# A two-layer Flamingo block on one core: the transfers that turn x, in rows of 2048 bytes and from GpSimd's queue

## The chip, the cores and the metric

The kernel runs on one core of a Trainium2 chip. The core has engines that work side by side: TensorE (PE) multiplies matrices, VectorE (DVE) and ScalarE (ACT) work elementwise, GpSimd (POOL) takes small rest work, and SyncE (SP) mostly asks for transfers. A transfer is asked for in the instruction stream of some engine and then carried out by 16 DMA engines that the core has. Each engine works through its own instructions in order, so an instruction that waits holds up all that are behind it.

The metric is the device time of one execution in microseconds (us), here the median of three runs. The profile is of one further execution, whose own time is given beside its span.

## The reference

Eight batches of 512 tokens, 512 features each, in float32 throughout. Two layers, each a gated cross-attention and a gated feed-forward part, all four with a layer norm in front and a residual around:

```python
x = x + tanh(g_xattn[0]) * L0_xattn(layernorm(x), ctx, Wq, Wg, bg, Wkv, Wo)      # "xa0"
x = x + tanh(g_ffn[0])   * L0_ffn(layernorm(x), proj1, b1, proj2, b2, gate_w)    # "ff0"
x = x + tanh(g_xattn[1]) * L1_xattn(layernorm(x), ctx, mask)                     # "xa1"
x = x + tanh(g_ffn[1])   * L1_ffn(layernorm(x), gate, gate_up, down, ...)        # "ff1"
```

- L0_xattn is linear attention with 16 heads over 64 context tokens, gated by a sigmoid: projections of 512 x 512.
- L0_ffn is a GELU network 512 to 2048 to 512 (its argmax over gate_w is thrown away).
- L1_xattn has no projections: softmax(x ctx^T / sqrt(512)) ctx, with a mask over the 64 context tokens.
- L1_ffn is a mixture of experts: a router of 32 logits a token, top 8, renormalised; the experts are merged into 8 groups of width 192, all of which are computed for each token and summed with the token's group weights.

## The kernel before

**Products.** Every large product is done by a scheme of seven block products in place of eight (Winograd's form of Strassen's), on blocks of half the rows and half the columns. The weights' block combinations are made once and kept in DRAM; those of x, called S, are made by four DVE sums per block (`token_combinations`, L686 to L689). `Up` (matmuls at L910) multiplies a layer's input by the first weights, with quarters of the turned x (`xnT`) or of S as the moving operand, 256 columns at a time. `SplitDown` (matmuls at L1105) does the second product of both feed-forward parts, with the scheme applied twice, and leaves its sums in PSUM; ACT copies them out (`part_ff_down`, L1132 and L1133) and DVE adds them up and on to x.

**Stages.** The stages run one after the other, each over the eight batches: xa0 (to about 377 us), ff0 (377 to 1085 us), and one stage for the second layer, in which each batch goes through xa1 and then ff1 (1085 us to the end, with a period of some 112 us). While PE works on one block, the next block is prepared, in steps of a generator that the main loop calls: `prep_ff0(b)`, or `prep_ff1(b)`, which is `cross_attention(b)` and then the norm, the router and its weights.

**The part that is changed.** A feed-forward product needs x normalised and turned, features on the partitions. `normed` (from L476) makes it:

1. DVE takes mean and variance of each quarter of the tokens (`bn_stats`, `st`, L487; `bn_aggr`, L488) and two small values from them (L490, L494).
2. POOL makes `rstd` (L495) and `nshift` (L497), 128x4 each.
3. ACT writes `xn` = x * rstd + nshift, a quarter of the tokens at a time (L507), with the columns regrouped.
4. DVE turns squares of 32 x 32 within each quarter of `xn`, in place (L562).
5. Sixteen transfers from SBUF to SBUF, for each group `q` of 32 partitions and each `l` of four column groups, carry a block of 32 partitions to partitions `32 l` and on of `xnT` (L580). Nothing of this is computed; it is a move across partitions.

The first blocks (xa0 and ff0_0) are turned on PE instead (L524, L528). The others, that is ff0_1 to ff0_7, and xa1 and ff1 of all eight batches, 23 in all, go by the sixteen transfers: 368 transfers of 64 KB. In the profile they are called `xnT_ff` and `xnT_xa` and have line L580, or L60 where a wrapper records the instruction in its written order.

Who uses `xnT`: the S sums (L686 to L689), `Up`'s products (L910), the scores of xa1 (`pst`, L729, 8 matmuls a batch), and the router's logits (`plt`, L789, 32 small matmuls a batch). From `plt` ACT copies the logits (`lT`, L797), PE turns them (`pl`, L800), DVE picks the top 8, and POOL and DVE make the group weights (`wg_e`, L825; `w`, L828; `pw`, L832).

**Order and queues.** The program is handed to a scheduler, which decides each engine's order by its own reckoning of durations, except where an engine is in the set `in_order`: then the instruction keeps its place in the written program. `with here("gpsimd")` puts GpSimd in that set for a statement. In ff0 the set holds SyncE alone; from the first step of the second layer on it is empty, and the scheduler orders SP too. SP asks for these in ff0 and ff1: weights in tiles of 256 KB into a ring of 16 tiles (`w_ff<-ff_up` for `Up`, `w_ff_down<-stream_ff` for `SplitDown`; `load_steps`, L1493 and L1498), x of the block after next (`x_ff<-x_ff`), the shares (group weights spread over rows, L850), the stores of the result, and the sixteen transfers per block:

```python
with here("gpsimd"):
    nc.sync.dma_start(out=xnT[ts(l, HD), :, q, :], in_=xn[ts(q, HD), :, ts(l, P)])
```

POOL asks for three transfers a batch in ff1 (`ctxd` twice, the context's rows, and `ctxdT`), and computes `rstd`, `nshift` and `wg_e`.

Of the kernel before, what the change touches and what calls it, by code (L numbers as in the profile page):

```python
# [30 lines left out]
P = 128  # L31
# [4 lines left out]
HD = 32  # L36
# [32 lines left out]
def flamingo_kernel(  # L69
# [405 lines left out]
    def normed(ph, b, tag, normed_part=lambda t: None):  # L475

        xb = xs[ph, b]
        by_products = ph == "xa0" or tag == "ff0_0"
        xnT = work.tile([P, NC, S] if ph == "xa0" else [P, NT, NC, P], F32, tag="xnT", name=f"xnT_{tag}")
        mv = small.tile([P, NT, 2], F32, tag="mv", name=f"mv_{tag}")  # L480
        held = ph == "ff0" and b > 1
        by_scalar = tag != "xa0_0"
# [32 lines left out]
        if by_products:  # L515

            def normed_tile(t):
                xn[t] = bank["xn"].tile([P, D], F32, tag="xn", name=f"xn_{tag}_{t}", bufs=2)
                norm(t, xn[t])

            def turn(t):
                pt = psum(f"pt_{tag}_{t}").rearrange("p (c q) -> p c q", q=P)
                for c in range(NC):
                    nc.tensor.transpose(pt[:, c, :], xn[t][:, ts(c, P)], ident)  # L524
                if ph == "xa0":
                    nc.scalar.copy(xnT[:, :, ts(t, P)], pt)
                else:
                    nc.scalar.copy(  # L528
                        xnT[:, t].rearrange("p q (c i) -> p c q i", c=NC),
                        pt.rearrange("p c (q i) -> p c q i", q=NC),  # L530
                    )

            if ph == "xa0" and b == 0:
                normed_tile(0)
                normed_tile(1)
                yield
                for t in range(NT):
                    turn(t)
                    if t + 2 < NT:
                        normed_tile(t + 2)  # L540
                    yield
                return xnT
            if ahead:
                normed_tile(0)
                yield
            for t in range(NT):
                if not ahead:
                    normed_tile(t)
                elif t + 1 < NT:
                    normed_tile(t + 1)  # L550
                turn(t)
                normed_part(t)
                yield
            return xnT


        at = (0, 2, 1, 3) if tag.startswith("ff1") else range(NT)
        xn = bank["xn"].tile([P, NT, D], F32, tag="xn", name=f"xn_{tag}")

        def squares(t):  # L560
            with here(*(["vector"] if ahead else [])):
                nc.vector.transpose(xn[:, at[t], :], xn[:, at[t], :])  # L562
            normed_part(t)

        for t in range(NT + 1):
            if t < NT:
                norm(
                    t,
                    xn[:, at[t], :].rearrange("p (l c e) -> p c l e", l=NC, c=NC),
                    lambda of: of.rearrange("p (c l e) -> p c l e", l=NC, c=NC),  # L570
                )
            if t > 0:
                squares(t - 1)
            if t % 2:
                yield
        yield
        for q in range(NC):
            for l in range(NC):
                with here("gpsimd"):
                    nc.sync.dma_start(out=xnT[ts(l, HD), :, q, :], in_=xn[ts(q, HD), :, ts(l, P)])  # L580
        yield
        if ph == "ff1":
            for _ in range(3):
# [3 lines left out]
    def features_of(ph, xnT):  # L587

        if ph == "xa0":
            return xnT.rearrange("p c (g i) -> p c g i", i=HD)  # L590
        return xnT.rearrange("p t q (c i) -> p c (t q) i", c=NC)

    turned = [dram.tile([P, NC, M], F32, tag=f"turned{b}", name=f"turned_{b}") for b in range(B)]

# [84 lines left out]
    def token_combinations(ph, b, xnT):  # L679

        s = work.tile([P, 4, 2, H2], F32, tag="S", name=f"S_{ph}_{b}", bufs=1)
        v = features_of(ph, xnT)
        a11, a12 = v[:, 0:2, 0:8], v[:, 2:4, 0:8]
        a21, a22 = v[:, 0:2, 8:16], v[:, 2:4, 8:16]
        to = s.rearrange("p k c (g i) -> p k c g i", i=HD)
        nc.vector.tensor_tensor(to[:, 0], a21, a22, ALU.add)  # L686
        nc.vector.tensor_tensor(to[:, 1], to[:, 0], a11, ALU.subtract)
        nc.vector.tensor_tensor(to[:, 2], a11, a21, ALU.subtract)
        nc.vector.tensor_tensor(to[:, 3], a12, to[:, 1], ALU.subtract)  # L689
        return s  # L690

    def prep_ff0(b):
        xb = xs["ff0", b]
# [9 lines left out]
    def cross_attention(b):  # L703
# [23 lines left out]
        for c in range(NC):  # L727
            for r in range(2):
                nc.tensor.matmul(  # L729
                    pst[ts(r, M), :],  # L730
                    lhsT=ctxT[:, c, :],
                    rhs=features_of("ff1", xnT)[:, c].rearrange("p (u r q) i -> p r u q i", u=2, r=2)[:, r],
                    start=c == 0,
                    stop=c == NC - 1,
                )
# [46 lines left out]
    def prep_ff1(b):  # L782
# [4 lines left out]
        for c in range(NC):  # L787
            for t in range(NT):
                nc.tensor.matmul(  # L789
                    plt[ts(t, E), :],  # L790
                    lhsT=router_sb[:, c, :],
                    rhs=features_of("ff1", xnT)[:, c, ts(t, NC)],
                    start=c == 0,
                    stop=c == NC - 1,
                )
# [92 lines left out]
    class Up(Unit):  # L888
# [6 lines left out]
        def product(self, m, p):  # L895
# [3 lines left out]
            for n in range(2):  # L899
                for c in range(2):  # L900
                    moving = {
                        1: v[:, c, 0:8],
                        2: v[:, 2 + c, 0:8],
                        4: v[:, 2 + c, 8:16],
                        5: s[:, 0, c, :],
                        6: s[:, 1, c, :],
                        7: s[:, 2, c, :],
                        3: s[:, 3, c, :],
                    }[m]
                    nc.tensor.matmul(  # L910
                        p[:, n, :],
# [742 lines left out]
```

## Time and profile before

| | |
|---|---|
| Time, median of 3 runs | 2036.1 us (2035.9 to 2041.35) |
| The profiled execution's own time | 2034.87 us |
| Its span; mean granted clock | 2033.1 us; 0.999 |
| PE busy | 2003.0 us, 99% |
| DVE busy | 1512.3 us, 74% |
| ACT busy | 646.7 us, 32% |
| POOL busy | 95.9 us, 5% |
| Queue q1 (what SP asks for) | 349616 packets, 479.79 MB, 73.6% |
| Queue q0 (what POOL asks for) | 1584 packets, 3.57 MB, 0.7% |

By stage, PE busy within each stretch (us):

| stretch | length | PE busy | DVE busy | DMA share |
|---|---|---|---|---|
| 60 to 350 (xa0) | 290.0 | 286.98 | 235.55 | 0.58 |
| 350 to 470 (into ff0) | 120.0 | 114.99 | 84.25 | 0.80 |
| 470 to 1085 (ff0) | 615.0 | 610.58 | 438.37 | 0.87 |
| 1085 to 1200 (first batch of layer two) | 115.0 | 108.46 | 89.22 | 0.82 |
| 1200 to 1980 (the other batches) | 780.0 | 778.86 | 595.92 | 0.80 |
| 1980 to 2033 (the end) | 53.0 | 47.09 | 41.98 | 0.55 |

How to read it: the busy time of an engine is the sum of its instructions' spans, with instructions that only ask for a transfer left out, so SP has no busy time at all and POOL's does not include its asking. Weight loads (PEld) lie beside matmuls. The share of a DMA queue is the time that its packets took over that of 16 engines for the whole span. Lines that name a group of instructions give line, engine, operation, and `out<-in` by the program's names; after `x` the number of instructions. A line of waits gives the engine and tile that waited, what ended the wait, and then the total in us, how many times, and the longest.

### The profile page before, as it was taken

The numbers are of one execution on the slowest core, as the hardware profiler recorded it, in microseconds if no ns is written. First come the engines' busy times: TensorE is split into PE (matmuls) and PEld (weight loads), VectorE is DVE, ScalarE is ACT, GpSimd is POOL, SyncE is SP. The second block draws the span as 40 slices with busy tenths as digits, with TensorE's granted clock in tenths as the row PEclk, the third lists the DMA queues.
The fourth block names the chain that finished last, engine by engine and source line by source line (L and its number), as shares of the span: only waits on it lengthen the run. The fifth ranks groups of instructions, "written<-read, shape, count | busy, mean of one in ns | idle before, by whom it ended". The sixth has DMA issues, their size and how long they took to land.

```text
span 2033.1 us, 34969 instructions
## 1 busy us (share of the span) xinstructions
PE 2003.0 (99%) x12428; PEld 1778.0 (87%) x12428; DVE 1512.3 (74%) x3012; ACT 646.7 (32%) x1294; POOL 95.9 (5%) x147
## 2 busy tenths in 40 slices
PE   9999999999999999999999999999999999999998
PEld 5888887889989899999988989898989888898988
DVE  4788888675857677777857787787778686876858
ACT  4533443323242424233233331313222232313122
POOL 3000000000000000000001010000001010100000
PEclk9999999999999999999999999999999999999999
DMA  7376556688979898989877869787878878786865
GB/s 211 127 217 189 178 156 175 231 304 276 341 236 347 264 341 260 314 291 297 305 245 233 294 217 294 230 291 212 294 238 266 262 234 273 215 288 211 277 203 172
DMA packets 357228, 508.79 MB, mean 250 GB/s; under 512 B 42944, under 2 KB 156768, under 8 KB 352960
## 3 DMA queue, kind: packets, MB, share of 16 engines
q1 hardware_dynamic: 349616, 479.79, 73.6%
q10 hardware_dynamic: 5856, 23.20, 3.1%
q0 software_dynamic: 1584, 3.57, 0.7%
q8 instruction: 100, 1.64, 0.3%
q14 instruction: 72, 0.59, 0.1%
HBM read 413.04 MB, written 69.27 MB: 237 GB/s over the span
## 4 chain that ended last, share of the span: by engine, by line
PE 47%; DVE 1%; DMA 1%; SPq 1%; ACT 0%; issue 0%; POOL 0%; DVEq 0%; POOLq 0%
PE x_ff L910 16%; PE w_ff L910 8%; PE x_ff_down L1105 7%; PE w_ff_down L1105 5%; PE z_ff L910 4%; PE z_ff_down L1105 2%; PE v_ff_down L1105 2%; PE pst L729 1%; PE pr L774 1%; SPq L580 0%; PE plt L789 0%; DMA w_ff<-ff_up 0%; DMA x_ff<-x_ff 0%; DVE xn_ff L562 0%; DVE st_xa L487 0%
## 5 line engine op out<-in xcount | busy, mean ns | idle before, releaser
L910 PE MATMUL w_ff<-S_ff,w_ff 128*128 128x256 f32 x1280 | 305.4, 380 | 2.7 <-DVE up_ff L1003 1.2
L910 PE MATMUL x_ff<-S_ff,w_ff 128*128 128x256 f32 x1280 | 304.0, 379 | 0.0
L910 PE MATMUL x_ff<-xnT_ff,w_ff 128*128 128x256 f32 x1280 | 299.1, 381 | 0.4 <-ACT u_ff L922 0.4
L922 ACT COPY u_ff<-x_ff 128x512 f32<-128x512 f32 x240 | 139.9, 583 | 463.4 <-PE x_ff L910 427.1
L910 PEld LDWEIGHTS w_ff<-S_ff,w_ff 128*128 128x128 f32 x1280 | 240.8, 190 | 39.5 <-DVE up_ff L1003 3.0
L910 PEld LDWEIGHTS x_ff<-S_ff,w_ff 128*128 128x128 f32 x1280 | 242.5, 190 | 34.2 <-ACT a_ff L60 0.8
L910 PEld LDWEIGHTS x_ff<-xnT_ff,w_ff 128*128 128x128 f32 x1280 | 240.4, 191 | 34.2 <-issue 1.8
L1105 PE MATMUL x_ff_down<-w_ff_down,split_ff_down 128*128 128x128 f32 x1344 | 161.8, 275 | 0.0
L1105 PEld LDWEIGHTS x_ff_down<-w_ff_down,split_ff_down 128*128 128x128 f32 x1344 | 155.8, 192 | 0.0
L910 PE MATMUL z_ff<-xnT_ff,w_ff 128*128 128x256 f32 x640 | 152.8, 380 | 0.0
L1119 DVE TENSOR_TENSOR part_ff_down<-part_ff_down 128x128 f32<-128x128 f32 x315 | 83.9, 285 | 73.2 <-ACT part_ff_down L1132 64.2
L910 PEld LDWEIGHTS z_ff<-xnT_ff,w_ff 128*128 128x128 f32 x640 | 119.9, 190 | 19.9 <-issue 4.5
L1105 PE MATMUL w_ff_down<-w_ff_down,split_ff_down 128*128 128x128 f32 x896 | 107.9, 275 | 0.0
L1105 PEld LDWEIGHTS w_ff_down<-w_ff_down,split_ff_down 128*128 128x128 f32 x896 | 103.9, 192 | 0.0
L970 ACT ACTIVATE a_ff<-a_ff,b_sb 128x256 f32<-128x256 f32 x128 | 58.1, 501 | 91.9 <-DVE a_ff L965 91.9
L1105 PE MATMUL w_ff_down<-w_ff_down,s_ff 128*128 128x128 f32 x672 | 83.1, 275 | 2.6 <-ACT part_ff_down L1132 2.6
L965 DVE TENSOR_TENSOR a_ff<-w_ff,u_ff 128x512 f32<-128x512 f32 x64 | 43.9, 685 | 53.8 <-ACT u_ff L922 53.2
L1105 PEld LDWEIGHTS w_ff_down<-w_ff_down,s_ff 128*128 128x128 f32 x672 | 80.1, 192 | 3.6 <-ACT part_ff_down L1132 2.8
L1003 DVE TENSOR_TENSOR up_ff<-w_ff,u_ff 128x512 f32<-128x512 f32 x96 | 65.6, 683 | 23.6 <-ACT u_ff L922 23.3
L1105 PE MATMUL x_ff_down<-w_ff_down,a_ff 128*128 128x128 f32 x672 | 82.8, 275 | 0.0
L1105 PEld LDWEIGHTS x_ff_down<-w_ff_down,a_ff 128*128 128x128 f32 x672 | 79.5, 192 | 0.4
L993 DVE SCALAR_TENSOR_TENSOR g_ff<-th_ff,x_ff 128x512 f32<-128x512 f32 x48 | 32.6, 680 | 63.2 <-ACT th_ff L992 63.2
(262 smaller groups left out, 3266.7 us busy)
## 6 DMA issues: line engine op xcount, KB each, us to landing
w_ff_down<-stream_ff SPq DMA_DIRECT2D x680, 256.0 KB
w_ff<-ff_up SPq DMA_DIRECT2D x560, 256.0 KB
stream_ff<-build_ff_down SPq DMA_DIRECT2D x49, 448.0 KB
x_ff<-x_ff SPq DMA_DIRECT2D x16, 1024.0 KB
share<-shares SPq DMA_DIRECT2D x64, 256.0 KB
xnT_ff<-xn_ff SPq DMA_DIRECT2D x240, 64.0 KB
ff_up<-build_ff_up SPq DMA_DIRECT2D x42, 256.0 KB
x_ff<-x_xa ACTq DMA_DIRECT2D x8, 1024.0 KB
```

The lines of the kernel that those rows point to most:

```text
L729: nc.tensor.matmul(pst[ts(r, M), :], lhsT=ctxT[:, c, :], rhs=features_of("ff1", xnT)[:, c].rearrange("p (u r q) i -> p r u q i", u=2, r=2) ...
L774: nc.tensor.matmul(pr[t], lhsT=eT[half, t // 2, :], rhs=c2[half, :], start=True, stop=True)
L910: nc.tensor.matmul(p[:, n, :], lhsT=w[:, c, ts(n, P)], rhs=moving, **self.mark(m, 2 * n + c),)
L922: nc.scalar.copy(self.s[m], p)
L965: nc.vector.tensor_tensor(h, p, s, ALU.add)
L970: nc.scalar.activation(h[:, n, :], p[:, n, :], AF.Gelu, bias=b1_sb[:, f : f + 1])
L993: nc.vector.scalar_tensor_tensor(g, th, 1.0, p, ALU.add, ALU.mult)
L1003: nc.vector.tensor_tensor(u, p, s, ALU.add)
L1105: nc.tensor.matmul(p[bank][:, place, :], lhsT=operand[k][:, c, :], rhs=w[at // 4][:, ts(at % 4, P)], start=bank not in opened, stop=True, ...
L1119: return lambda: nc.vector.tensor_tensor(m(k), m(k), m(by), ALU.add)
```

## The change

`xn` and `xnT` are laid out anew so that what one of the sixteen transfers reads in a partition lies in one row of 2048 bytes, and what it writes too; before, it was four rows of 512 bytes at each end. The token quarter moves from the first to the second place in `xnT` ([column group, token quarter, 128]) and in `xn`. All that reads `xnT` or S is rewritten to find the same elements: the views of `features_of`, the S sums, the moving operands of `Up`, the scores and the logits. S, for blocks outside of xa0, takes the order of `xnT`. The sixteen transfers are asked for with `nc.gpsimd.dma_start` in place of `nc.sync.dma_start`; the `here("gpsimd")` around them now applies to the engine that asks. No product, sum or transfer is added or left out.

```diff
--- before.py
+++ after.py
@@ -476,7 +476,7 @@
 
         xb = xs[ph, b]
         by_products = ph == "xa0" or tag == "ff0_0"
-        xnT = work.tile([P, NC, S] if ph == "xa0" else [P, NT, NC, P], F32, tag="xnT", name=f"xnT_{tag}")
+        xnT = work.tile([P, NC, S] if ph == "xa0" else [P, NC, NT, P], F32, tag="xnT", name=f"xnT_{tag}")
         mv = small.tile([P, NT, 2], F32, tag="mv", name=f"mv_{tag}")
         held = ph == "ff0" and b > 1
         by_scalar = tag != "xa0_0"
@@ -526,7 +526,7 @@
                     nc.scalar.copy(xnT[:, :, ts(t, P)], pt)
                 else:
                     nc.scalar.copy(
-                        xnT[:, t].rearrange("p q (c i) -> p c q i", c=NC),
+                        xnT[:, :, t].rearrange("p q (c i) -> p c q i", c=NC),
                         pt.rearrange("p c (q i) -> p c q i", q=NC),
                     )
 
@@ -555,18 +555,18 @@
 
 
         at = (0, 2, 1, 3) if tag.startswith("ff1") else range(NT)
-        xn = bank["xn"].tile([P, NT, D], F32, tag="xn", name=f"xn_{tag}")
+        xn = bank["xn"].tile([P, NC, NT, P], F32, tag="xn", name=f"xn_{tag}")
 
         def squares(t):
             with here(*(["vector"] if ahead else [])):
-                nc.vector.transpose(xn[:, at[t], :], xn[:, at[t], :])
+                nc.vector.transpose(xn[:, :, at[t], :], xn[:, :, at[t], :])
             normed_part(t)
 
         for t in range(NT + 1):
             if t < NT:
                 norm(
                     t,
-                    xn[:, at[t], :].rearrange("p (l c e) -> p c l e", l=NC, c=NC),
+                    xn[:, :, at[t]].rearrange("p l (c e) -> p c l e", c=NC),
                     lambda of: of.rearrange("p (c l e) -> p c l e", l=NC, c=NC),
                 )
             if t > 0:
@@ -577,7 +577,7 @@
         for q in range(NC):
             for l in range(NC):
                 with here("gpsimd"):
-                    nc.sync.dma_start(out=xnT[ts(l, HD), :, q, :], in_=xn[ts(q, HD), :, ts(l, P)])
+                    nc.gpsimd.dma_start(out=xnT[ts(l, HD), q], in_=xn[ts(q, HD), l])
         yield
         if ph == "ff1":
             for _ in range(3):
@@ -587,8 +587,8 @@
     def features_of(ph, xnT):
 
         if ph == "xa0":
-            return xnT.rearrange("p c (g i) -> p c g i", i=HD)
-        return xnT.rearrange("p t q (c i) -> p c (t q) i", c=NC)
+            return xnT.rearrange("p c (t q i) -> p c t q i", q=NC, i=HD)
+        return xnT.rearrange("p q t (c i) -> p c t q i", c=NC)
 
     turned = [dram.tile([P, NC, M], F32, tag=f"turned{b}", name=f"turned_{b}") for b in range(B)]
 
@@ -679,15 +679,20 @@
     def token_combinations(ph, b, xnT):
 
         s = work.tile([P, 4, 2, H2], F32, tag="S", name=f"S_{ph}_{b}", bufs=1)
-        v = features_of(ph, xnT)
-        a11, a12 = v[:, 0:2, 0:8], v[:, 2:4, 0:8]
-        a21, a22 = v[:, 0:2, 8:16], v[:, 2:4, 8:16]
-        to = s.rearrange("p k c (g i) -> p k c g i", i=HD)
+        if ph == "xa0":
+            v = features_of(ph, xnT).rearrange("p c t q i -> p c t (q i)")
+            a11, a12, a21, a22 = (v[:, ts(h, 2), ts(r, 2)] for r in range(2) for h in range(2))
+            to = s.rearrange("p k c (t i) -> p k c t i", t=2)
+        else:
+            a11, a12, a21, a22 = (xnT[:, :, ts(r, 2), ts(h, 2 * HD)] for r in range(2) for h in range(2))
+            to = s.rearrange("p k c (q t i) -> p k (c q) t i", q=2, t=2)
         nc.vector.tensor_tensor(to[:, 0], a21, a22, ALU.add)
         nc.vector.tensor_tensor(to[:, 1], to[:, 0], a11, ALU.subtract)
         nc.vector.tensor_tensor(to[:, 2], a11, a21, ALU.subtract)
         nc.vector.tensor_tensor(to[:, 3], a12, to[:, 1], ALU.subtract)
-        return s
+        if ph == "xa0":
+            return to.rearrange("p k c t (q i) -> p k c t q i", i=HD)
+        return to.rearrange("p k q t (c i) -> p k c t q i", c=2)
 
     def prep_ff0(b):
         xb = xs["ff0", b]
@@ -729,7 +734,7 @@
                 nc.tensor.matmul(
                     pst[ts(r, M), :],
                     lhsT=ctxT[:, c, :],
-                    rhs=features_of("ff1", xnT)[:, c].rearrange("p (u r q) i -> p r u q i", u=2, r=2)[:, r],
+                    rhs=features_of("ff1", xnT)[:, c].rearrange("p (u r) q i -> p r u q i", r=2)[:, r],
                     start=c == 0,
                     stop=c == NC - 1,
                 )
@@ -789,7 +794,7 @@
                 nc.tensor.matmul(
                     plt[ts(t, E), :],
                     lhsT=router_sb[:, c, :],
-                    rhs=features_of("ff1", xnT)[:, c, ts(t, NC)],
+                    rhs=features_of("ff1", xnT)[:, c, t],
                     start=c == 0,
                     stop=c == NC - 1,
                 )
@@ -899,13 +904,13 @@
             for n in range(2):
                 for c in range(2):
                     moving = {
-                        1: v[:, c, 0:8],
-                        2: v[:, 2 + c, 0:8],
-                        4: v[:, 2 + c, 8:16],
-                        5: s[:, 0, c, :],
-                        6: s[:, 1, c, :],
-                        7: s[:, 2, c, :],
-                        3: s[:, 3, c, :],
+                        1: v[:, c, 0:2],
+                        2: v[:, 2 + c, 0:2],
+                        4: v[:, 2 + c, 2:4],
+                        5: s[:, 0, c],
+                        6: s[:, 1, c],
+                        7: s[:, 2, c],
+                        3: s[:, 3, c],
                     }[m]
                     nc.tensor.matmul(
                         p[:, n, :],
```

## The prediction

> **What bounds the kernel now.** I read the page's engine totals first, then the waits of PE, then the groups of the moved transfers, then the stretches by stage.
>
> ```profile
> span 2033.1 us, 34969 instructions
> PE 2003.0 (99%) x12428; PEld 1778.0 (87%) x12428; DVE 1512.3 (74%) x3012; ACT 646.7 (32%) x1294; POOL 95.9 (5%) x147
> q1 hardware_dynamic: 349616, 479.79, 73.6%
> q0 software_dynamic: 1584, 3.57, 0.7%
> ```
>
> PE is busy for 2003.0 of 2033.1 us, and its instructions number the same after the change. So no DMA saving is worth anything by itself; only a PE gap that closes or opens counts. Queue q1, which holds what SP asks for, is busy 73.6% on average: not the limit, though it can be late in places. The waits of PE from 385 us on (before that no x goes by the changed transfers):
>
> ```profile
> PE v_ff_down L1105 <- DMA w_ff_down<-stream_ff: 6.1, 3, 3.0
> PE w_ff_down L1105 <- ACT part_ff_down L1132: 2.6, 1, 2.6
> PE plt L789 <- issue: 1.4, 3, 0.8
> PE w_ff L910 <- DVE up_ff L1003: 1.2, 1, 1.2
> PE w_ff L910 <- DVE x_ff L776: 1.2, 1, 1.2
> PE plt L789 <- DMA xnT_ff<-xn_ff: 0.6, 1, 0.6
> ```
>
> These and smaller ones sum to 14.6 us. Besides, nine matmuls at 1093.5-1097 took 631 ns in place of 379, in the one stretch with a granted clock of 0.99: 9 x 0.25 = 2.3 us. **The whole possible gain is 14.6 + 2.3 = 17 us.** The 6.1 us are the weight waits at 433 (2.6), 623 (0.5) and 1090 us (3.0). What SP did ahead of the first shows in its timeline:
>
> ```profile
> 403.86 0.32 SPq L60 DMA_DIRECT2D w_ff_down<-stream_ff  x1
> 404.23 4.41 SPq L60 DMA_DIRECT2D ff_up<-build_ff_up  x7
> 408.75 11.89 SPq L60 DMA_DIRECT2D xnT_ff<-xn_ff  x16
> 420.74 1.02 SPq L60 DMA_DIRECT2D w_ff_down<-stream_ff  x2
> ...
> 428.39 5.40 SPq L60 DMA_DIRECT2D w_ff_down<-stream_ff  x7
> ```
>
> SP asks for nothing else during 11.89 us of x; the down weights go out late, and PE waits at 433.42. Likewise 16 x issues at 1074.54-1086.10 stand ahead of the down weights of 1087.32, for which PE waits at 1089.76.
>
> **The change, part by part.** (1) *Issues.* 23 preparations (ff0_1 to 7, and xa and ff of eight batches) x 16 = 368 issues leave SP and join POOL.
>
> ```profile
> L60 SPq DMA_DIRECT2D xnT_ff<-xn_ff x128: 585/599/1986, 408.7 to 1085.5; - x128
> L580 SPq DMA_DIRECT2D xnT_ff<-xn_ff x112: 586/599/1609, 1188.1 to 1870.1; - x112
> ```
>
> On SP, 599 ns each, 0.645 from start to start: 16 take 10.3 us or more, and SP gets back 368 x 0.645 = 237 us. On POOL the nearest row is the context load (64 rows of 2 KB; the moved ones have 32):
>
> ```profile
> L60 POOL DMA_DIRECT2D ctxd<-in_ctx x16: 523/556/603, 947.7 to 1770.3; - x16
> DMA to landing us min/median/max: 2.8/4.2/6.3
> ```
>
> So 16 x 0.56 = 9.0 us of issuing a preparation, 206 us in all on an engine busy for 95.9. What then stands behind it on POOL: in a batch of ff1 the next block's rstd_xa and nshift_xa (1302.14, 1.2 us), which now come after the 16 of xnT_ff, near 1309-1310. ACT uses them at 1313.17 (xn_xa), so some 2 us of slack cover it; without the cover ACT's xn_xa, and behind it the copy of the router's logits, are late by the excess. wg_e (1319.24) follows still later.
>
> (2) *Rows.* In the trace's packet records those of 512 B took 27 ns (median; mean 30.9), of 2048 B 84 (mean 98): 47104 x 30.9 becomes 11776 x 98, 1455 to 1154 us over 16 engines, 91 to 72 each, 0.9% of their share. Hidden; worth nothing but a little earlier landing.
>
> (3) *Layouts.* The moving operand now has 128 B runs with other strides. A matmul from xnT (strided already) takes 381 or 379 ns and one from S (contiguous) 380 or 379; DVE's S sums 681 and transposes 704, ACT's xn 805, with the same element counts after. I cost this at 0. If strides cost 5 ns on each of the 1280 + 640 matmuls from xnT, it would be 10 us; the equal rows exclude that.
>
> (4) *ff0, 377-1085 us.* PE's order stays. POOL can issue when the transposes end (near 390 us for ff0_1) with landing by 399-406; first use is 428.9: hidden, with 20 us of cover. SP's 11.89 us go away before 433. I take both waits as closed: **-2.6 - 0.5 = -3.1 us** (ends 0 and -3.1).
>
> (5) *Turn from ff0 to ff1, 970-1100.* Here SP without its 16 issues asks for weights and x about 10 us sooner. The waits of the cluster at 1087-1097 (0.8 plt, 3.0 w_ff_down, 0.7 small ones, and the 2.3 us of slow matmuls, which follow the gaps) sum to 6.8; 10 us of head start exceed each of them, and I take **-6.0** (ends 0 and -6.8). At 1009.87 PE waits 2.6 us for a copy behind four xn_xa in a row on ACT (1009.06-1011.99); in the built order two of that bank's copies come between them, so that at most two stand together: half, **-1.3** (ends 0 and -2.6). The gaps at 1065.68 and 1190.6 (1.2 each) hang on DVE: 0. Against it: the scheduler, reckoning with the earlier SP, moves DVE's statistics st_xa_0 14 to 25 instructions ahead, before the sum at 974.5. They need x_ff, which SP asked for at 977.67 and which let DVE go at 986.19, 8.5 us after. Without the 10.4 us of issues at 964.65 it goes out at 967-972, so landing is 975.6-980: DVE, in order, blocks for 1 to 5 us, with a_ff and s_ff sums behind it that PE multiplies by. st_xa_1 is moved alike, before 1075.8, with x asked for at about 1071-1075. DVE is busy only 74%, so most is made up: **+1.5 for both** (ends 0 and +8).
>
> (6) *Steady ff1, seven batches.* A period of 112 us has PE busy for 111.43 to 112.00, so almost no gain is left. The new order wants xnT_xa at about 1269, with POOL able to send it from 1212: 40 us of cover. The tight one is plt, which needs all 16 landings:
>
> ```profile
> 1299.32 0.70 DVE L562 STREAM_TRANSPOSE xn_ff<-xn_ff 128x512 f32<-128x512 f32 x1
> 1313.44 1.08 PE L789 MATMUL plt<-xnT_ff,router_sb 128*32 128x128 f32 x32
> ```
>
> The last transpose ends at 1300.0, plt is three matmuls earlier after the change (0.65 us), so landing has 12.75 us. A queue has eight completion lanes in the built order, so the ninth issue waits for the first to land. With landing L from issue, sixteen are down at the greater of 15 x 0.56 + L and, in two rounds, 2L + 7 x 0.56: 11.2 us for L = 2.8, 12.5 for 4.2, 16.5 for 6.3. By the median row plt is just in time. Before, plt waited 1.15 us over three batches; I take the same after: **0** (ends -1.2, and 7 x 3.7 = +26).
>
> *The rule against it.* The Trainium skill ("DMA: Bandwidth & Descriptors", section "SWDGE vs HWDGE vs iDMA") calls descriptors written by software on GpSimd the slower set-up; the page's first table gives about 1 us to the first byte against 0.6. The trace's nearest rows: plt starts 1.8 to 3.1 us after SP's last x issue ends, so 2.4-3.7 from its start, against 4.2 on POOL; yet the issue itself is shorter, 0.556 to 0.599. Before, plt starts 13.4 us after the last transpose, with waits of at most 0.6: so long do SP's sixteen take. With the rule's 0.4 us for each of two rounds of lanes, and no credit for issuing, POOL's take 14.2: 1.5 us late in each of seven batches, **+10 in place of 0**. I take the row, since L = 4.2 already holds that latency and 0.56 the shorter issue; the rule's answer stays in the range. The page "SBUF - State Buffer" ("Who interferes with whom") further says that GpSimd's descriptor writing is shut out while DVE runs in a two-port mode. DVE's 512-element rows take 650 to 704 ns whatever the operation, none near half, and the context loads kept to 523-603 ns beside DVE at 78%: I add nothing for it.
>
> **Sum:** -3.1 - 6.0 - 1.3 + 1.5 + 0 = -8.9 us against a profiled execution of 2034.87 (span 2033.1 and 1.8 around it), so 2026.0. That execution lies 1.2 us under the median of the three runs, 2036.1; on the median's footing, 2027.2, said as 2027.
>
> **The rivals.** *Late landing on POOL* ends on the other side. Place: plt in each ff1 batch; stalls begin at L = 4.4 us (2 x 4.4 + 3.9 = 12.7) and eat the whole gain at 5.0, where 13.9 is 1.2 too late, x 7 = 8. At L = 6.3, the slowest context load, 3.7 x 7 = 26 us: 2053. For it: 64 KB from only 32 partitions into 32 others may be slower than the context's 64, and DMA share is 0.8. Against: SP's x landed in under 3.7 us in that traffic, with four times the packets. *Waits only change places*: SP is ahead, but w_ff_down waits for ring tiles that PE frees, or DVE's early statistics cost +8 where SP gave -9: 2035. For it: the ring holds 16 tiles however early SP is free. Against: at 408-420 SP was plainly late. *All goes well*: every gap named shuts and DVE doesn't block: -13 to -17, 2019-2023. *Nothing of what it says*, that transfers stay with SP, is excluded: the built order has them on POOL.
>
> **How the numbers follow.** My forecast (2023-2031) 0.47; waits change places (2031-2042) 0.20; late landing (above 2042) 0.18; all goes well (below 2023) 0.15. About 6 us (0.3%) is what a measurement of this kernel can tell from no change, so faster means below 2030: all of the best case and 0.42 of my forecast, whose last us lies above, 0.57. Slower means above 2042: 0.18. The same is the rest, 0.25. The range leaves out 0.1 at each side, the lower part of the best case and the upper part of late landing: 2021 to 2046.
>
> **What would show it.** Right: no w_ff_down wait on stream_ff at 433 and 1090; POOL's xnT issues near 0.56 us; plt waits under 0.5 us a batch; a DVE wait of 1-5 us for x_ff near 975; matmuls from xnT at 379-381 ns. Wrong: plt <- DMA xnT_ff of over 1 us in each batch, POOL issues over 0.7 us, ACT's xn_xa waiting for nshift_xa with the logits behind it, or PE waits on DVE that outgrow 2 us at 975-1100.

## The result: slower, and the profile after

The changed kernel takes 2048.35 us (median of 7 runs, 2041.27 to 2058.18) against 2035.9 (7 runs, 2032.2 to 2041.35). The ratio over all runs is 1.0067, with a 95% interval of 1.0045 to 1.0089 (the medians alone give 1.0061). The forecast was 2027.

The head of the page of the changed kernel, to be held against that of the kernel before (busy times, share of the span, number of instructions; then packets, MB and share of two DMA queues):

```profile
span 2044.1 us, 35151 instructions
PE 2006.4 (98%) x12428; PEld 1781.7 (87%) x12428; DVE 1508.6 (74%) x3012; ACT 648.5 (32%) x1294; POOL 281.1 (14%) x515
q1 hardware_dynamic: 296624, 455.65, 71.2%
q0 software_dynamic: 13360, 27.71, 4.9%
```

The transfers moved as the change says: q0 has the 24 MB more that q1 lost. q1's share fell by 2.4 points, but q0's rose by 4.2. The span grew by 11.0 us all the same. PE is busy 3.4 us longer for the same 12428 matmuls, so the other 7.6 us are idle time of PE. What it waited for after 385 us:

```profile
PE plt L794 <- DMA xnT_ff<-xn_ff: 16.7, 8, 3.7
PE x_ff L915 <- ACT u_ff L927: 2.4, 1, 2.4
PE pw L837 <- DVE w L833: 1.2, 1, 1.2
PE v_ff_down L1110 <- ACT a_ff L975: 1.1, 1, 1.1
PE x_ff_down L1110 <- DVE split_ff_down L1095: 0.9, 1, 0.9
```

(Lines from L910 on are five higher than before: L910 is L915, L789 is L794.) The 6.1 us of waits for `w_ff_down<-stream_ff` are gone, as forecast. In their place stands one line that the kernel before had with 2.0 us: the router's logits wait for x, now in every one of the eight batches.

How the two kernels ran against each other is seen best by a landmark that both have: the end of the last DVE transpose (L562) of each batch's ff1 block, read from the timelines of DVE.

| batch | before, us | after, us | after is ahead by | plt then waited, after |
|---|---|---|---|---|
| 1 | 1188.03 | 1182.47 | 5.6 | 2.3 |
| 2 | 1300.02 | 1297.91 | 2.1 | 0.6 |
| 3 | 1411.75 | 1410.08 | 1.7 | 3.4 |
| 4 | 1523.99 | 1526.70 | -2.7 | 0.5 |
| 5 | 1635.57 | 1638.79 | -3.2 | 1.1 |
| 6 | 1747.36 | 1751.47 | -4.1 | 1.9 |
| 7 | 1859.38 | 1864.96 | -5.6 | 3.7 |
| end | 2033.1 | 2044.1 | -11.0 | |

The changed kernel was 5.6 us ahead when the steady part began, with 3.1 us already lost at the plt of batch 0. Then it lost 16.6 us in seven batches.

One of these batches in the timeline of GpSimd's queue (start, length, instruction; in brackets the idle time before it and what ended it), and then of SyncE's in the same time:

```profile
1527.25 3.99 POOL L60 DMA_DIRECT2D xnT_ff<-xn_ff  x8 [8.22 <-PE x_ff L915]
1532.08 3.92 POOL L60 DMA_DIRECT2D xnT_ff<-xn_ff  x8 [0.84 <-DMA xnT_ff<-xn_ff]
1536.02 1.27 POOL L495 TENSOR_TENSOR rstd_xa<-var_xa,neg_half 128x4 f32<-128x4 f32 x1
1537.37 0.46 POOL L497 TENSOR_TENSOR nshift_xa<-nshift_xa,rstd_xa 128x4 f32<-128x4 f32 x1
```

```profile
1525.67 8.84 SPq L1498 DMA_DIRECT2D w_ff_down<-stream_ff  x6
1535.91 2.04 SPq L1503 DMA_DIRECT2D w_ff<-ff_up  x2
```

Eight issues of 0.50 us, a pause until the first of them has landed, eight more. The last issue starts at 1535.5 and plt starts at 1539.42, 12.7 us after the transposes of 1526.70. Of the seven batches this is the one with the shortest wait at plt, 0.5 us. SyncE asks for six weight tiles (1.5 MB) in the midst of it. The landings of the ff1 blocks on GpSimd, batches 1 to 7:

```profile
L60 POOL DMA_DIRECT2D xnT_ff<-xn_ff x112: 498/498/558, 1183.0 to 1875.8; - x112
...
  DMA xnT_ff<-xn_ff: 8.2, 10
...
  ACT xn_xa L507: 21.6, 6
  PE plt L794: 13.6, 7
...
DMA to landing us min/median/max: 3.2/4.3/6.5
```

The second line is GpSimd's idle time until an earlier transfer of its own has landed, before the ninth issue or one close behind it: its queue has eight completion lanes, each free again when its transfer has landed. The two lines after it are who waited for these landings: PE for 13.6 us, and ACT, whose next xn reuses the buffer that the transfers read, for 21.6. ACT is let go by the same landings; no wait of PE hangs on it.

The 3.4 us of longer busy time come after the longest of these waits. The windows around the plt of batch 3 (us, PE busy, then other engines; PEclk is the granted clock):

```profile
1420.00:1426.00 6.00, 2.61 (x24) 2.03 (x26) 1.74 (x3) 0.69 (x2) 3.16 (x6) 1.00 0.72 199
1426.00:1432.00 6.00, 6.00 (x45) 4.80 (x37) 4.76 (x21) 4.67 (x11) 0.00 (x0) 0.72 0.19 48
1432.00:1438.00 6.00, 6.00 (x30) 5.18 (x29) 4.28 (x11) 0.76 (x2) 4.39 (x7) 1.00 0.65 174
```

After 3.4 us of idling the clock is 0.72 over the next 6 us: 0.28 x 6 = 1.7 us on top of the wait. The same happens at batches 1 and 7 (waits of 2.3 and 3.7), three times in all, 5.1 us; the kernel before had it once (10 us at 0.83, behind the wait of 3.0 at 1090 us), 1.7 us. The difference is the 3.4 us. With the 7.6 us of idle time the 11.0 us of span are accounted for.

### The profile page after: what moved, and what is told of

It is laid out like the page before. It is cut to its first block, busy times and chain, and to the rows that moved or that the text cites. A ratio compares the mean times of both kernels' runs of the same rounds, so it can differ in the third digit from the quotient of the medians.

```text
span 2044.1 us, 35151 instructions
## 1 busy us (share of the span) xinstructions
PE 2006.4 (98%) x12428; PEld 1781.7 (87%) x12428; DVE 1508.6 (74%) x3012; ACT 648.5 (32%) x1294; POOL 281.1 (14%) x515
## 4 chain that ended last, share of the span: by engine, by line
PE 85%; DVE 5%; DMA 5%; ACT 1%; POOL 1%; issue 1%; SPq 0%; DVEq 0%; ACTq 0%; POOLq 0%
PE x_ff L915 24%; PE x_ff_down L1110 12%; PE w_ff L915 12%; PE w_ff_down L1110 9%; PE z_ff L915 6%; PE z_ff_down L1110 4%; PE v_ff_down L1110 4%; DMA xnT_ff<-xn_ff 3%; PE x_xa_down L1031 2%; PE x_q L915 2%; PE x_g L915 1%; POOL xnT_ff L60 1%; PE w_xa_down L1031 1%; PE w_g L915 1%; PE w_q L915 1%
## 5 line engine op out<-in xcount | busy, mean ns | idle before, releaser
L915 PE MATMUL x_ff<-S_ff,w_ff 128*128 128x256 f32 x1280 | 304.8, 380 | 2.4 <-ACT u_ff L927 2.4
L915 PE MATMUL w_ff<-S_ff,w_ff 128*128 128x256 f32 x1280 | 303.9, 380 | 0.5 <-DVE a_ff L970 0.3
L915 PE MATMUL x_ff<-xnT_ff,w_ff 128*128 128x256 f32 x1280 | 299.0, 382 | 0.0
L915 PEld LDWEIGHTS x_ff<-S_ff,w_ff 128*128 128x128 f32 x1280 | 242.3, 190 | 36.5 <-ACT u_ff L927 2.8
L915 PEld LDWEIGHTS w_ff<-S_ff,w_ff 128*128 128x128 f32 x1280 | 240.9, 190 | 37.4 <-issue 2.7
L915 PEld LDWEIGHTS x_ff<-xnT_ff,w_ff 128*128 128x128 f32 x1280 | 242.4, 192 | 33.6 <-issue 1.4
L915 PE MATMUL z_ff<-xnT_ff,w_ff 128*128 128x256 f32 x640 | 153.1, 380 | 0.0
L60 POOL DMA_DIRECT2D xnT_ff<-xn_ff x240 | 118.9, 502 | 183.0 <-PE x_ff L915 84.5
L495 POOL TENSOR_TENSOR rstd_ff<-var_ff,neg_half 128x4 f32<-128x4 f32 x15 | 15.9, 1062 | 898.9 <-DVE nshift_ff L494 898.9
L915 PEld LDWEIGHTS z_ff<-xnT_ff,w_ff 128*128 128x128 f32 x640 | 119.8, 190 | 20.7 <-issue 5.3
```

The source lines that it names most:

```text
L60: made = f(*args, **kw)
L495: nc.gpsimd.tensor_tensor(rstd, var, neg_half, ALU.pow)
L915: nc.tensor.matmul(p[:, n, :], lhsT=w[:, c, ts(n, P)], rhs=moving, **self.mark(m, 2 * n + c),)
```

## Experiments

All kernels differ from the changed one only as shown. Three theories are weighed. LANES: sixteen transfers pass eight completion lanes in two rounds, so that a slow landing counts twice. TRAFFIC: landings on GpSimd are late because SyncE's weight loads go over the same DMA engines. LAYOUT: the new rows and strides cost. Each ratio is to the kernel before, run on the same chip beside it.

| kernel | median, us | before, us | ratio (95%) | plt waits, us | other main PE waits |
|---|---|---|---|---|---|
| rows alone, SyncE | 2031.49 | 2033.53 | 0.9991 (0.9981-1.0000) | 0.4 | weights 6.7 |
| queue alone, rows of 512 | 2065.98 | 2033.53 | 1.0157 (1.0126-1.0188) | 26.2 | |
| SyncE held by small transfers | 2063.49 | 2033.53 | 1.0147 (1.0127-1.0166) | 27.9 | |
| half on SyncE | 2031.10 | 2033.53 | 0.9993 (0.9983-1.0002) | 8.6 | |
| half of the weights' bytes | 2027.64 | 2033.20 | 0.9972 (0.9958-0.9985) | 5.3 | |
| plt later | 2063.85 | 2033.20 | 1.0144 (1.0120-1.0168) | 3.1 | pw 16.4, u_ff 8.9 |
| ff1 on SyncE | 2024.09 | 2033.20 | 0.9955 (0.9938-0.9972) | 0.3 | |
| half on SyncE, plt later | 2026.23 | 2033.20 | 0.9957 (0.9941-0.9974) | 0 | u_ff 7.2 |
| half on ScalarE | 2085.38 | 2036.16 | 1.0267 (1.0237-1.0296) | 0.8 | u_ff 36.7 |
| only ff0 on GpSimd | 2031.83 | 2036.16 | 0.9982 (0.9972-0.9992) | 0.8 | pw 3.3 |

### The two halves of the change, each alone

The rows alone:

```diff
-                    nc.gpsimd.dma_start(out=xnT[ts(l, HD), q], in_=xn[ts(q, HD), l])
+                    nc.sync.dma_start(out=xnT[ts(l, HD), q], in_=xn[ts(q, HD), l])
```

> The new rows and layouts alone: rows of 2048 bytes, asked for by SyncE as before. The order of every engine is that of the kernel before. Theory LANES (plt is late because sixteen transfers on GpSimd's queue go through eight completion lanes in two rounds, so a landing counts twice): plt waits as before, under 2 us over all batches, ratio 0.997 to 1.002. Theory TRAFFIC (plt is late because SyncE, freed of its sixteen issues, asks for weights in the same moment, and the transfers land late among them): the same, since SyncE still spends the time. Theory LAYOUT (the new strides or rows themselves cost): the full loss, ratio about 1.006, and matmuls from xnT longer than 379 to 381 ns.

The queue alone, put into the kernel before:

```diff
-                    nc.sync.dma_start(out=xnT[ts(l, HD), :, q, :], in_=xn[ts(q, HD), :, ts(l, P)])
+                    nc.gpsimd.dma_start(out=xnT[ts(l, HD), :, q, :], in_=xn[ts(q, HD), :, ts(l, P)])
```

> The queue alone: the four rows of 512 bytes, asked for by GpSimd. The order of every engine is that of the changed kernel. LANES: plt waits of 15 us or more in all, since four times the packets land no earlier: ratio 1.006 to 1.012. TRAFFIC: the same or more, 1.006 to 1.012, as SyncE is just as free. LAYOUT: ratio 1.000.

The first waits of PE with the rows alone, and with the queue alone:

```profile
PE v_ff_down L1110 <- DMA w_ff_down<-stream_ff: 6.7, 3, 3.1
PE w_ff_down L1110 <- ACT part_ff_down L1137: 1.7, 1, 1.7
```

```profile
PE plt L789 <- DMA xnT_ff<-xn_ff: 24.5, 7, 5.0
PE x_ff L910 <- ACT u_ff L922: 2.4, 1, 2.4
```

LAYOUT falls: with the rows alone the ratio is 0.9991, matmuls from xnT take 379 ns as before, and the old weight waits are all there. The queue costs 1.57% with the old rows and 0.67% with the new ones, so the rows win back a little over half of what the queue loses: an issue on GpSimd takes 498 ns in place of 548, and the 256 packets of 4096 bytes that its queue moved in the ff1 block of batch 4 took 204 ns on average in place of 231 (from the trace's packet records). On SyncE the same rows win 0.09%, with an interval of 0 to 0.19. The queue is the loss. The time of the queue alone lay above what either theory had said (1.012 at most).

### SyncE held as before

```diff
+        paced = dram.tile([NC * NC, HD, 8], F32, tag="paced", name=f"paced_{tag}", bufs=2)
         for q in range(NC):
             for l in range(NC):
                 with here("gpsimd"):
                     nc.gpsimd.dma_start(out=xnT[ts(l, HD), q], in_=xn[ts(q, HD), l])
+                nc.sync.dma_start(out=paced[NC * q + l], in_=xn[ts(q, HD), l, 0, 0:8])
```

> The changed kernel, with SyncE asking for sixteen small transfers (32 rows of 32 bytes, from xn to a scratch in DRAM) where it had asked for x; GpSimd still carries x. SyncE is held for some 10 us per block as before, so no weights go out in that time. TRAFFIC: x on GpSimd lands sooner (median near 3 us in ff1), plt waits shrink from 16.7 to under 6 us in all; the weight waits at 433 and 1090 us come back (some 5 us): ratio about 1.000 to 1.003. LANES: sixteen are still two rounds; plt waits stay above 10 us, ratio 1.007 to 1.010 with the weight waits on top.

The landings of the ff1 blocks, batches 1 to 7, and the waits of PE:

```profile
DMA to landing us min/median/max: 2.0/4.5/7.1
```

```profile
PE plt L796 <- DMA xnT_ff<-xn_ff: 20.0, 6, 5.4
PE plt L796 <- issue: 7.9, 2, 4.3
```

TRAFFIC in the form that was written down is wrong: with SyncE held, the landings come no sooner (4.5 against 4.3 us), the plt waits grow from 16.7 to 27.9, and the ratio, 1.0147, lies above both bands. The order within a block tells why. In the block of batch 4 (first issue at 1531.5) the sixteen landings took 5.0, 4.9, 4.6, 4.5, 4.4, 4.1, 4.0, 3.9, then 3.0, 3.5, 3.2, 3.7, 4.4, 4.8, 5.7, 6.3 us. SyncE's small issues ran from 1530.9 to 1537.2, its five weight tiles went out at 1537.35. The landings shorten while SyncE is held, and lengthen once the pent-up tiles go out, which is when the last transfers, those that plt waits for, are on their way. This fits weights that delay x, which the next trial tests; holding SyncE only moves them, and adds sixteen small transfers. The trial couldn't tell the theories apart as it was meant to.

### Half of the weights' bytes

In the last stage a row of 1024 bytes is loaded of each weight tile in place of 2048, and the products use the loaded half twice, so that what they compute is not the reference's; the instructions are the same in number, and the order of PE, DVE, ACT and GpSimd is unchanged.

```diff
+                    n = min(n, 2 * P) if u.ph == "ff1" else n
                     nc.sync.dma_start(out=t[:, 0:n], in_=flat[:, at : at + n])
...
-            nc.sync.dma_start(out=t, in_=store[u.ph, u.i, SLOT[m]])
+            if u.ph == "ff1":
+                nc.sync.dma_start(out=t[:, 0], in_=store[u.ph, u.i, SLOT[m]][:, 0])
+            else:
+                nc.sync.dma_start(out=t, in_=store[u.ph, u.i, SLOT[m]])
...
-                        lhsT=w[:, c, ts(n, P)],
+                        lhsT=w[:, 0 if self.ph == "ff1" else c, ts(n, P)],
...
-                        rhs=w[at // 4][:, ts(at % 4, P)],
+                        rhs=w[at // 4][:, ts(at % 2 if self.ph == "ff1" else at % 4, P)],
```

> The changed kernel, with only half of each weight tile loaded in the last stage (1024 of 2048 bytes a row; the products use that half twice, so they compute something else with the same number of matmuls). The order of PE, DVE, ACT and GpSimd is that of the changed kernel. TRAFFIC: the landings on GpSimd come down from a median of 4.7 us for xnT_ff and 6.5 for xnT_xa to 3 or less, and the plt waits of the eight batches from 16.7 us to under 4: ratio 0.993 to 0.999. LANES, with a software queue that is slow in itself: landings stay above 4, plt waits above 10 us, ratio 1.003 to 1.008.

The last stage in the changed kernel and here (the last three numbers are the clock, the DMA share and GB/s):

```profile
1200.00:1984.00 784.00, 772.52 (x4754) 689.96 (x4754) 587.17 (x1157) 200.83 (x409) 140.31 (x260) 0.99 0.81 247
1200.00:1984.00 784.00, 783.38 (x4827) 700.54 (x4826) 597.61 (x1175) 205.31 (x417) 137.60 (x260) 1.00 0.54 158
```

The landings of the ff1 blocks of batches 1 to 7 and who waited for them, and the first waits of PE over all batches:

```profile
L60 POOL DMA_DIRECT2D xnT_ff<-xn_ff x112: 496/496/558, 1187.0 to 1863.6; - x112
...
  DMA xnT_ff<-xn_ff: 0.4, 1
...
  ACT xn_xa L507: 1.7, 3
  PE plt L794: 0.6, 1
...
DMA to landing us min/median/max: 1.8/2.4/4.1
```

```profile
PE plt L794 <- DMA xnT_ff<-xn_ff: 5.3, 2, 4.6
PE x_ff L915 <- ACT u_ff L927: 2.4, 1, 2.4
```

With the DMA share of 1200 to 1984 us down from 0.81 to 0.54, the median landing falls from 4.3 to 2.4 us, GpSimd's waits for its own lanes shrink from 8.2 to 0.4, and PE waits 0.6 us in place of 13.6 for batches 1 to 7. The sixteen still go in two rounds; but a landing of 2.4 us is over before the eight issues (4.0 us) are, so the second round costs nothing. The rest of the 5.3 us belongs to batch 0, where the ff0 weights' traffic is still whole. GpSimd's queue is thus not slow in itself; in the presence of the weights it is. xnT_xa's median went from 6.5 to 5.4 us only, where 3 or less was expected: so much of the expectation was wrong, and what slows those landings was not followed up.

### One round of lanes

```diff
-                    nc.gpsimd.dma_start(out=xnT[ts(l, HD), q], in_=xn[ts(q, HD), l])
+                    queue = nc.sync if l % 2 else nc.gpsimd
+                    queue.dma_start(out=xnT[ts(l, HD), q], in_=xn[ts(q, HD), l])
```

> The changed kernel with half of the transfers (l = 1 and 3) asked for by SyncE, half by GpSimd: eight on each, one round of lanes on GpSimd, and two issuers at once. LANES: issue 4 us and one landing of 4 to 6: all down some 9 us after the transposes, plt waits under 2 us in all; ratio 0.994 to 0.998. TRAFFIC: SyncE is held for only 5 us, weights still come in between; plt waits of 5 to 10 us stay, ratio 1.000 to 1.004.

And with ScalarE in SyncE's place:

```diff
+                    queue = nc.scalar if l % 2 else nc.gpsimd
```

> The changed kernel with half of the transfers (l = 1 and 3) asked for by ScalarE, half by GpSimd; SyncE stays as free as in the changed kernel, so the weights' traffic is that of the changed kernel, but no queue has a second round of lanes. If the second round is what doubles the late landings: all down 4 + 4.5 = 8.5 to 10 us after the transposes in place of 12 to 15, GpSimd's ninth-issue gap gone. If traffic alone sets it, whatever the rounds: 12 us or more from the transposes to plt. ScalarE pays some 8 x 0.6 = 5 us of issuing per block, on an engine that is busy 27% in this stage; the scheduler places plt for the shorter landing, so that some wait for it stays: ratio 0.998 to 1.004.

With eight on each of two queues, plt follows the last transpose by 7.9 to 9.5 us (SyncE and GpSimd, all eight batches), in place of 12.7 to 15.9 in batches 1 to 7. With ScalarE, SyncE is as free as in the changed kernel. GpSimd's landings of the ff1 blocks, batches 1 to 7:

```profile
DMA to landing us min/median/max: 4.3/5.2/7.0
```

They are as slow as ever, or slower, and yet GpSimd's transfers are all down 8.1 to 10.2 us after its first issue (batches 1 to 7), in place of 11.8 to 15.0, and plt hardly waits (0.8 us in all, on a PE that is itself late by then). This does not show LANES, though: the trial takes away the second round and eight issues of 0.50 us on GpSimd together, and the issues alone are 4.0 of the 4.5 us that the transfers are down earlier on average. What the second round costs is read from the changed kernel itself. Its pauses for a lane in batches 1 to 7 were 2.0, 0.5, 0.6, 0.8, 0.4, 1.2 and 2.7 us, the 8.2 shown above. Had each batch come earlier by its pauses, with landings as long as they were, some 5.7 of the 13.6 us of plt waits would be left (an estimate), half of it in batch 3, where GpSimd also paused 2.8 us without a semaphore to wait for (see the end). So the lanes turn long landings into more than half of the waits; without long landings they cost nothing, as the half weights show.

With ScalarE the loss went elsewhere. First what ACT waited for from 1000 us on, then PE:

```profile
ACT u_ff L928 <- DMA xnT_ff<-xn_ff: 53.6, 8, 8.0
ACT build_sums_ff_down L1170 <- DMA xnT_xa<-xn_xa: 46.2, 7, 8.5
```

```profile
PE x_ff L916 <- ACT u_ff L928: 36.7, 19, 4.9
PE pw L838 <- DVE w L834: 1.6, 5, 0.6
```

ScalarE stands still up to 8.5 us at its own x issues, and the copies behind them are the ones that PE's next product wants. The expectation had priced the eight issues (5 us a block on an engine with room) and not what waits behind them: 1.0267 in place of 0.998 to 1.004. The half on SyncE kept 8.6 us of plt waits, since the scheduler, which places plt by its own reckoning of the landing, put it 22 matmuls earlier in batches 2 to 7; its waits are those that TRAFFIC had said (5 to 10), and its ratio, 0.9993, lies just under TRAFFIC's band (the interval reaches into it) and above that of LANES.

### plt at a later place

```diff
-            for _ in range(3):
+            for _ in range(7 if tag.startswith("ff1") else 3):
                 yield
...
+        with here("tensor"):
             for c in range(NC):
...
-        for _ in range(4):
+        for _ in range(0):
             yield
         pw = psum(f"pw_{b}")[0 : G * NT, 0:P]
```

> The changed kernel with plt nine matmuls (1.95 us) later on PE in batches 2 to 7 and eight later in batch 1: two steps of the generator come before plt that came before pw, and plt keeps its written place. If the loss of the changed kernel is plt's place before its transfers, and nothing else, the waits shrink by 1.95 us each where they were that long: of 2.3, 0.6, 3.4, 0.5, 1.1, 1.9, 3.7 some 3.6 us stay, the time falls by 10 us, ratio 0.999 to 1.003. If GpSimd's queue costs in another place, the ratio stays at 1.005 or above.

(As the diff shows, it is four steps that were moved, not two: plt comes 18 matmuls later in batches 2 to 7, not nine, and pw 44 later.) The first waits of PE after 385 us:

```profile
PE pw L838 <- DVE w L834: 16.4, 8, 2.1
PE x_ff L916 <- ACT u_ff L928: 8.9, 4, 3.0
PE z_ff_down L1111 <- DMA w_ff_down<-stream_ff: 4.1, 1, 4.1
PE plt L60 <- DMA xnT_ff<-xn_ff: 3.1, 1, 3.1
```

The plt waits are gone but for batch 0, and the time is worse by far: the waits turn up 2.1 us at a time at pw, whose router work on DVE now comes in behind the sums for the second product. The expectation (0.999 to 1.003) missed. With pw moved too, this is no trial of plt's place alone. Next a delay with half of the transfers on SyncE. Two steps are moved in place of four. plt comes 24 matmuls later than with the half alone, not twelve, which in batches 1 to 7 is within two matmuls of its place in the changed kernel, and pw keeps its own place:

```diff
+            for _ in range(5 if tag.startswith("ff1") else 3):
...
+        for _ in range(2):
```

> Half of the transfers on each queue, as tried before, and plt pinned twelve matmuls (2.6 us) later than there in batches 1 to 7. The plt waits of that run (8.6 us with the one of w_ff_down) shrink to under 2, and nothing else moves: ratio 0.994 to 0.997, below both kernels. If the later plt only moves the wait to pw or to the shares behind it, the ratio stays near 0.999.

The only waits of PE after 385 us that are left:

```profile
PE x_ff L917 <- ACT u_ff L929: 7.2, 5, 2.4
```

It came to 0.9957, as expected. With plt where the changed kernel has it, two issuers of eight are thus enough to take its waits away. That the room between landing and pw decides if plt can be moved is what these two suggest; it is not shown.

### The tight blocks back on SyncE

```diff
+                    queue = nc.sync if tag.startswith("ff1") else nc.gpsimd
```

> The changed kernel with only the eight blocks that plt waits for (ff1) put back on SyncE; ff0 and xa1 stay on GpSimd, all rows of 2048 bytes. LANES and TRAFFIC: plt waits as in the kernel before (under 2 us), the weight waits of ff0 gone (3 us): ratio 0.995 to 0.998. If GpSimd's queue costs in another place: ratio above 1.000.

The first waits of PE after 385 us:

```profile
PE x_ff L916 <- ACT u_ff L928: 2.4, 1, 2.4
PE pw L838 <- DVE w L834: 1.1, 1, 1.1
PE v_ff_down L1111 <- ACT a_ff L976: 1.1, 1, 1.1
```

0.9955: faster than the kernel before and the changed one, as expected. GpSimd's queue costs nothing where x has tens of microseconds of room (landings of xnT_xa still have a median of 6.4 us), and SyncE has the time that its weights needed. With only ff0 on GpSimd:

```diff
+                    queue = nc.gpsimd if ph == "ff0" else nc.sync
```

> Rows of 2048 bytes; only the seven blocks of ff0 are asked for by GpSimd, the sixteen of the last stage by SyncE. It tells how the gain of the kernel with only the ff1 blocks on SyncE (0.9955) divides. The weight waits at 433 and 623 us vanish (3.1 us) and those at the turn to the last stage stay (some 5 us with the slow matmuls after them): ratio 0.997 to 0.9985, between the rows alone (0.9991) and 0.9955. If it reaches 0.9955, xa1's transfers give nothing.

0.9982, within the expected band. So of the 0.45% the rows give about 0.1, ff0's queue about 0.1, and the rest comes with xa1's transfers, as far as intervals of 0.1 to 0.2 to either side tell. The weight wait at the turn to the last stage, 3.0 us, shrank to 1.2 already; a wait of 3.3 us for pw in batch 0 replaced it.

## Why the prediction was wrong

Step by step:

- **(1) Issues.** Right: 498 ns on GpSimd, 0.50 from start to start (0.56 was taken). The work behind them on POOL (rstd_xa, nshift_xa) ended in time, at 1537.8 in the batch shown. That ACT's xn_xa would wait for the landings, since they read its buffer (21.6 us), was not seen, and cost PE nothing.
- **(2), (3) Rows and layouts.** Right on the time: 379 to 382 ns a matmul, and the rows alone are worth some 0.1%. The 0.9 points of DMA share that the rows were to save did not come: on GpSimd's queue packets are of 4096 bytes with either rows, and the shares of q1 and q0 together rose from 74.3 to 76.1%.
- **(4) ff0.** Right: the waits at 433 and 623 us are gone, 3.1 us.
- **(5) The turn.** Right in its sum, not in its parts. Up to the transposes of batch 1 the steps (4) and (5) gave -3.1 - 6.0 - 1.3 + 1.5 = -8.9; measured 5.6 us ahead with 3.1 lost at plt of batch 0, by the mechanism of (6) in a batch that (6) did not count: 8.7 without it. DVE waited 5.5 us for x in two places (1 to 5 each was said), PE at most 2.4 for what it held up. The wait of 2.6 at 1012 us vanished whole, where 1.3 was said; three waits of 0.9 to 1.1 at 976 to 991 us came new. The slow matmuls after 1093 us were worth 1.7, not 2.3, as the nine durations overlap.
- **(6) Steady ff1.** This failed: "By the median row plt is just in time ... I take the same after: 0". The waits of batches 1 to 7 are 13.6 us, 1.9 a batch, and bring slow clocks of 3.4 us net, which (6) put at nothing, though (5) had seen slow matmuls behind gaps.

The mechanism in (6) was the right one: plt waits for sixteen landings that come in two rounds. Its terms were off in size, and the 1.9 us can be taken apart (an estimate from the blocks of batches 1 to 7):

- The first issue starts 0.55 us after the last transpose. The formula left this out.
- PE wants plt 12.2 us after the transpose, not 12.75. The new order has it six matmuls earlier, not three (42 ahead of pw, where the kernel before has 36): 0.55 us.
- Sixteen were down 11.8 to 15.0 us after the first issue, 13.4 on average, where 12.5 was put in (12.6 by its own formula): 0.9 us. The median landing was nearly the one forecast, 4.3 us, but the landings went from 3.2 to 6.5, and the long ones held up the ninth issue too. The pause of 2.8 us in batch 3 is 0.4 of the 0.9.
- plt starts some 0.2 us after the last landing. Of the whole, 0.25 us of slack between 12.5 and 12.75 goes off.

So the two small terms are over half of the waits, and they made all seven batches late. With them as forecast, the same landings would have left some 7 us of waits, in four of the batches: the median alone would still have been too little, since a batch that lands early gives nothing back. (This says what the sum lacked. It doesn't add to the share of the lanes given above: a wait can be shortened from either end.)

The rival *late landing on POOL* has the place, plt in each ff1 batch, and the sign. That the time fell into its band (above 2042) is in part luck: its formula stalls from a landing of 4.4 us on, and with the first and last landing of each batch put in it gives some 4 of the 13.6 us. It too lacked the late first issue, the smaller window and the clock.

The Trainium skill's rule against the change ("DMA: Bandwidth & Descriptors", "Specifications": 0.4 us later to the first byte on GpSimd; an estimate of +10 us for the seven batches, where 16.6 were lost) had the right sign, but not the cause: with half of the weights' bytes the same queue lands in 2.4 us. That is close to the 2.0 us + bytes / 436e3 of the same page ("Anatomy of one DMA — SWDGE (gpsimd) path"), which gives an estimate of 2.15 us for 64 KB. What came on top in the median, 1.9 us, went with the weights' bytes. The case in which DVE shuts GpSimd out isn't needed for any of it: the issues kept to 498 to 558 ns. (The prediction's 650 to 704 ns for DVE's 512-element rows leaves out some of 541 to 926 ns in other places; none is near half.)

## What to carry to other kernels

A transfer moved to another queue is judged where its landing is wanted soonest, not by what it frees: put the blocks with room on the idle queue and leave the tight ones where they were. Where the cover is as long as the median landing, count every step from the last producer to the consumer, price the spread, since only late landings count, and add the second round where a landing outlasts the issues of the first. And an engine that issues transfers waits in them with all that is behind: GpSimd could afford that here, ScalarE could not.

## What the runs showed of the hardware beyond that

- A wait can cost more than its length. Three waits at plt of 2.3, 3.4 and 3.7 us were each followed by a stretch of 3.4 us at a granted clock of 0.50 (1198.4 to 1201.8 us at batch 1), which loses 1.7 us. One of 3.1 us (1080 us), one of 2.4 (1063 us) and the shorter ones (0.5 to 1.9) were not; with half on SyncE, one of 1.9 us was (0.72 over 1746 to 1752 us) and one of 2.1 was not. The Trainium skill ("TensorE: Matmul & The Clock Gate", "What's actually happening") has the clock at half after an idle window of some 3.4 us, on a free-running counter, until a busy window of that length has passed. The 3.4 us at half clock agree, and a free-running window fits waits of like length that differ. That waits of 1.9 and 2.3 us were enough does not agree, if PE's waits alone count as idle; the runs don't show what else does.
- On GpSimd's queue the packets were of 4096 bytes, 256 for sixteen transfers of 64 KB, whether the rows were 512 or 2048 bytes; on SyncE's they were as long as the rows.
- In the block of batch 3, GpSimd paused 2.8 us between its first and second issue with no semaphore to wait for, in the changed kernel and in three of the trials alike. A packet of 16 KB on the instruction queue lies in that pause (1412.1 us). That it is the cause wasn't tried.
